# Attention and Mamba on one core: the result added up by DMA, the input normalised on ScalarE, weights folded once, 144 columns of a product on GpSimd

## The chip, the cores and the metric

The kernel runs on one core of a Trainium2 chip. A core has five engines, each with its own queue of instructions that it takes strictly in order: TensorE (PE in the profile; PEld is its loading of weights), VectorE (DVE), ScalarE (ACT), GpSimd (POOL) and SyncE (SP), which here only issues DMAs. The metric is the device time of one execution in microseconds (us). The kernel before took 8720.66 us, the median of three runs (8711.55 to 8721.42).

## The reference

The input x has 8 samples of 512 channels and 48 x 48 = 2304 positions, in float32. Two layers are added to it:

```
x = x + L0(gn(x))       # linear causal attention, 8 heads of 64 channels
x = x + L1(gn(x))       # four Mamba blocks over 4 groups of 128 channels
```

`gn` normalises groups of 16 channels by their mean and variance over all positions. L0 projects the normalised input to q, k and v and takes a running sum over the positions. L1 goes through the four channel groups one after the other; each gets the fused output of the one before added to its input:

```
x_i   = spx[i] + prev                       # 128 channels
xp, z = split(x_i @ Wi.T)                   # 256 channels each
xs    = silu(causal_conv4(xp))              # one filter of 4 taps per channel
delta, B, C = projections of xs             # 16 states
h_t   = exp(delta*A) * h_{t-1} + (delta*xs) * B_t     # the scan, per channel and state
y     = (sum_n h_t C_t + D*xs) * silu(z);  x_m = y @ Wo.T
fused = sigmoid(mean x_i) * x_i + sigmoid(mean max) * max(x_i, x_m)
prev  = fused                               # and the block's output
```

So the result for a channel group is x1 (the input plus attention) plus fused.

## The kernel before, in words

**Tiling.** The positions are cut into 6 chunks of LC = 384 columns. The attention of a sample is done in 4 passes of 128 output channels, 6 chunks each: 8 x 4 x 6 = 192 chunks (`chunk`). The Mamba part has 32 blocks (8 samples x 4 groups), each of 6 jobs (`Job`): 192 jobs. A job has 8 slots, and a slot treats 2 of the 16 states for 128 of the 256 channels (two groups of 64 channels, two states each, so that 128 partitions are full): 1536 slots.

**A slot.** The tile u holds 4 rows of 384 columns per partition. First u = B x (delta xs) is formed: DVE makes the first LC - TAIL = 256 columns (`product`, L867, from dxp, a copy in PSUM that ACT made at L840), POOL the last TAIL = 128 (`last_product`, L856). Then DVE scans the four rows (`scan`, L888), each with a decay that ACT has just computed into a PSUM bank (`decay`, L877). POOL multiplies all of u by C (`weigh`, L900), and PE sums the states into yp (`gather`, L916). The decays are made up to three ahead of the scans (`DEPTH`). POOL's part of the product is issued two slots ahead and DVE's one; u has five buffers.

**A job's preparation** (`prepare`): convolution (PE, L693) with the folded weights wk, SiLU on ACT, projections, delta by Softplus (ACT, L764). Delta is stored to DRAM (`spread`, L773), then multiplied in place by xs on POOL in two halves (L805), and stored again. From DRAM both are read back in the layout of the slots (dr, dxr), as are B and C (L797). The first half of L805 overwrites what the first store reads, so it waits for that DMA.

**Weights** (`weights`): before each of the 32 blocks the kernel loads the projection wi and the four taps, spread over the partitions, as wk, and POOL multiplies wk by wi for each tap (L539, 128 instructions), one every three half slots. ACT makes the table av (L536, L540).

**Passing on** (`pass_on`): when a block is done, chunk by chunk, fused is put together: ACT scales the stored maximum fu and the input xi (L654, L655), POOL adds them (L662) and adds fused to the next block's input (L667, or ACT at L665 where a new sample begins). Then POOL adds fused to x1, which was loaded as xo (L670), and the sum is stored to `out`. The last block of stream 1 has a path of its own on DVE (L630).

**Attention chunk.** In the first pass of a sample (o = 0) the chunk's input xn is loaded from x (`fetch`, issued when the chunk before starts), normalised on POOL in four instructions (L317), used by PE for the projections (L293), and stored for the three later passes, which load it normalised. The attention's output plus x (x1) is stored to a scratch tensor in DRAM.

**Order.** The schedule is written out by hand. Time is counted in half slots. Two streams of blocks (even and odd samples) take turns. At every half slot `beside` advances the side tasks that are due, each a generator whose `yield` says how many half slots later, or at which one, it goes on; `at(j)` means j half slots from the start of the chunk, and chunks start 16 half slots apart (11 in the ramp). `save` puts a store in a list, and `flush` issues it on SP at least two half slots later. The place of an instruction in its engine's queue is thus fixed when the program is built; when it runs depends on the waits of all that stands before it.

Of the kernel before, what the change touches and what calls it, by code (L numbers as in the profile page):

```python
# [9 lines left out]
F32 = mybir.dt.float32  # L10
BF16 = mybir.dt.bfloat16
AF = mybir.ActivationFunctionType
ALU = mybir.AluOpType
# [8 lines left out]
SLOTS = 8  # L22
TAIL = 128
BANKS = 6
# [26 lines left out]
def attention_then_mamba_kernel(  # L51
# [206 lines left out]
    def fetch(m):  # L258

        if m == len(parts):  # L260
            return
        b, o, c = parts[m]
        if (o, c) == (0, 0):
            xns[b] = dpool.tile([512, L], F32, tag="xn", name=f"xn_{b}", bufs=B)
            x1s[b] = dpool.tile([512, L], F32, tag="x1", name=f"x1_{b}", bufs=B)
        xn = apool.tile([P, 4, LC], F32, tag="xn", name=f"xn_{b}_{o}_{c}", bufs=2)
        src = (x[b] if o == 0 else xns[b]).rearrange("(t p) l -> p t l", p=P)
        nc.sync.dma_start(out=xn, in_=src[:, :, c * LC : (c + 1) * LC])
        fetched[m] = xn
# [3 lines left out]
    def chunk(m):  # L273
# [35 lines left out]
        if o == 0:  # L309
            yield at(-4), 0  # L310
            while b not in norms or m not in fetched:
                yield "1w", 0
            xn, norm = fetched.pop(m), norms[b]
            for ct in range(4):
                if ct:
                    yield at(ct - 4), 0
                nc.gpsimd.tensor_scalar(  # L317
                    xn[:, ct, :],
                    xn[:, ct, :],
                    norm[:, 0, ct : ct + 1],  # L320
                    norm[:, 1, ct : ct + 1],
                    ALU.mult,
                    ALU.add,
                )
            save(xns[b].rearrange("(t p) l -> p t l", p=P)[:, :, cols], xn)
# [165 lines left out]
        if c + 1 == NC:  # L491
# [4 lines left out]
            done[b, o] = norm  # L496

    class Stream:

# [10 lines left out]
        def weights(self):  # L510
# [6 lines left out]

            wk = wpool.tile([P, 4, 256], F32, tag=f"wk{z}", name=f"wk_{n}")
            nc.sync.dma_start(
                out=wk.rearrange("p k d -> p (k d)"), in_=wconv[s].to_broadcast([P, 1024])  # L520
            )
# [14 lines left out]
            nc.scalar.activation(av, av, AF.Exp)  # L536
            for k in range(4):
                yield "3", 0
                nc.gpsimd.tensor_tensor(wk[:, k, :], wk[:, k, :], wi[:, 0:256], ALU.mult)  # L539
            nc.scalar.mul(av, av, -1.0)  # L540
            self.scaled = True

        def move_on(self):

            if self.b is not None and self.s < 3:
                self.s += 1
                self.fresh = False
            else:
                self.b, self.s = self.samples.pop(0), 0
                self.fresh = True  # L550
            self.ready = 0
            self.block += 1
            self.n = f"{self.b}_{self.s}"
            self.state = small.tile(
                [P, 2, NS // 2, 2], F32, tag=f"state{self.z}", name=f"state_{self.n}", bufs=1
            )
            self.fsum = small.tile([P, NC], F32, tag=f"fsum{self.z}", name=f"fsum_{self.n}", bufs=1)
            self.fm = dpool.tile([P, L], F32, tag="fm", name=f"fm_{self.n}")
            self.w = self.coming

        def pass_on(self):
# [39 lines left out]
            def loads(c):  # L601
                fu = xb = xa = None
                cols = slice(c * LC, (c + 1) * LC)
# [3 lines left out]
                if old is not None:  # L607
                    fu = mpool.tile([P, LC], F32, tag="fu", name=f"fu_{old[2]}_{c}")
                    nc.sync.dma_start(out=fu, in_=old[3][:, cols])
                    xa = mpool.tile([P, LC], F32, tag="xo", name=f"xo_{old[2]}_{c}")  # L610
                    nc.sync.dma_start(out=xa, in_=x1s[old[0]][old[1] * P : (old[1] + 1) * P, cols])
                return fu, xb, xa

            if last and self.z:
# [19 lines left out]
                return  # L634
            now = loads(0)
            for c in range(NC):
# [12 lines left out]
                cols, icols = slice(c * LC, (c + 1) * LC), slice(3 + c * LC, 3 + (c + 1) * LC)  # L649
                fu, xb, xa = now  # L650
                if not last:
# [8 lines left out]
                if old is not None:  # L660
# [5 lines left out]
                    elif not last:  # L666
                        nc.gpsimd.tensor_tensor(xi[:, icols], xb, fu, ALU.add)  # L667
                    self.ready = c + 1
                    yield "1", 0
                    nc.gpsimd.tensor_tensor(xa, xa, fu, ALU.add)  # L670
                    save(out[old[0], old[1] * P : (old[1] + 1) * P, cols], xa)
                self.ready = c + 1

    class Job:
# [6 lines left out]
        def prepare(self):  # L681
# [120 lines left out]

            for h in range(2):
                yield "1", 0
                nc.gpsimd.tensor_tensor(delta[:, h, :], delta[:, h, :], xs[:, h, :], ALU.mult)  # L805
            yield "2", 0
            xsrc = spread("xscr")
# [227 lines left out]
    def begin(latest):  # L1035

        nonlocal begun, put
        while counted and begins[counted[0]] - 4 <= half_no[0]:
            tasks.append(Task(statistics(counted.pop(0))))
        while put < len(parts) and times[put] - 6 <= half_no[0]:  # L1040
            put += 1
            heads.append(Task(chunk(put - 1), before=heads[-1] if heads else None))
# [226 lines left out]
```

## Time and profile before

| | |
|---|---|
| median of three runs | 8720.66 us (8711.55 to 8721.42) |
| the profiled execution's own time | 8723.09 us |
| its span in the profile | 8721.0 us |
| mean granted TensorE clock | 0.964 |
| DMA | 1643 MB, 188 GB/s, SP's queue 69.1% of 16 engines |
| longest waits on SP's queue | 1187 us for L805, 832 us for L670 |
| POOL's waits at L805 | 235 us for the store of delta (80 times), 56 us booked on another DMA |

The span is the time from the first to the last instruction that the profile shows. A busy time is the time in which an engine had an instruction in work, and since PE pipelines its matmuls, its busy time is an upper bound. A line of a group says: line of the kernel, engine, operation, output and inputs with their shapes, count, busy time and mean duration of one in ns, and the idle time of the engine just before these instructions with what ended it. A line of the waits says who waited for whom, how long in total, how often, and the longest. A line of the stretches gives a window, its length, and the busy time of PE, PEld, DVE, ACT and POOL with the number of instructions, then the granted clock, the share of the DMA engines and GB/s.

### The profile page before, as it was taken

Reading aid. Unit: us, or ns where it says so; the run is one execution under the profiler, and the core shown is the slowest. Engines: PE = TensorE matmul, PEld = TensorE weight load, DVE = VectorE, ACT = ScalarE, POOL = GpSimd, SP = SyncE. Lnnn points to the kernel's source line nnn. Section 1 sums busy time; section 2 is a strip of 40 time slices with the busy share of each in tenths; the row PEclk is TensorE's granted clock in tenths of the full one; section 3 lists DMA queues with packets and bytes.
Section 4 is the critical chain, followed back from the end, with each engine's and each line's share of the span. In section 5 each row is a group of like instructions: output and inputs, shape, how many; then the busy total and the mean of one; then the engine's idle time right before and its main releaser. Section 6 shows DMA issues by size and latency. Waiting matters only on the chain. (4 is left out here: it accounts for less than half of the span.)

```text
span 8721.0 us, 124881 instructions
## 1 busy us (share of the span) xinstructions
PE 7774.7 (89%) x36482; PEld 3714.5 (43%) x36482; DVE 8072.2 (93%) x11078; ACT 6852.0 (79%) x14500; POOL 7834.3 (90%) x4343
## 2 busy tenths in 40 slices
PE   7899999988899999998889999999889999999965
PEld 4444444444444444444444444444444444444422
DVE  2899999999899999998899999999889999999998
ACT  2788888777788888877778888887777888888876
POOL 1789999999999999998998999998999889999998
PEclk9999999999999999999999999999999999999987
DMA  5667777776766777776676777776666667766665
GB/s 183 168 178 190 196 198 197 191 191 189 195 188 190 193 200 199 197 189 191 187 193 186 193 190 197 196 197 187 188 185 194 188 188 190 189 188 185 183 165 146
DMA packets 1002924, 1643.11 MB, mean 188 GB/s; under 512 B 138592, under 2 KB 797312, under 8 KB 1002240
## 3 DMA queue, kind: packets, MB, share of 16 engines
q1 hardware_dynamic: 1002240, 1635.13, 69.1%
q8 instruction: 290, 4.75, 0.2%
q14 instruction: 394, 3.23, 0.1%
HBM read 1309.06 MB, written 325.58 MB: 187 GB/s over the span
## 5 line engine op out<-in xcount | busy, mean ns | idle before, releaser
L888 DVE TENSOR_TENSOR_SCAN u<-bank,u 128x385 f32<-128x385 f32 (+1 forms) x6144 | 5455.4, 938 | 327.4 <-ACT bank L877 288.3
L900 POOL TENSOR_TENSOR u<-u,C 128x1536 f32<-128x1536 f32 x1536 | 4892.7, 3185 | 345.6 <-DVE u L888 186.9
L877 ACT ACTIVATE bank<-dr,av 128x385 f32<-128x385 f32 (+1 forms) x6144 | 3405.1, 578 | 671.0 <-DVE u L888 575.2
L916 PE MATMUL yp<-u,cst 128*64 128x384 f32 x12288 | 2417.7, 515 | 343.9 <-POOL u L900 259.6
L856 POOL TENSOR_TENSOR u<-B,dxr 128x512 f32<-128x512 f32 x1536 | 1969.9, 1283 | 17.5 <-DMA dxr<-xscr 15.4
L867 DVE TENSOR_TENSOR u<-B,dxp 128x1024 f32<-128x1024 f32 x1536 | 1835.0, 1195 | 9.7 <-ACT dxp L840 9.7
L293 PE MATMUL bank<-xn,wq_sb 128*128 128x384 f32 x4608 | 1725.8, 519 | 74.2 <-DVE u L888 33.0
L916 PEld LDWEIGHTS yp<-u,cst 128*64 128x64 f32 x12288 | 780.7, 139 | 1557.9 <-issue 871.9
L693 PE MATMUL bank<-xi,wk 128*128 128x384 f32 x3072 | 1110.7, 505 | 198.6 <-ACT kl L390 108.7
L293 PEld LDWEIGHTS bank<-xn,wq_sb 128*128 128x128 f32 x4608 | 867.4, 199 | 842.4 <-DVE u L888 140.0
L693 PEld LDWEIGHTS bank<-xi,wk 128*128 128x128 f32 x3072 | 558.8, 192 | 761.4 <-ACT kl L390 211.6
L805 POOL TENSOR_TENSOR delta<-delta,xs 128x384 f32<-128x384 f32 x384 | 385.7, 1005 | 361.8 <-DMA dscr<-delta 234.6
L305 ACT ACTIVATE ex<-bank,bqkv_sb 128x384 f32<-128x384 f32 x384 | 221.5, 577 | 505.3 <-PE bank L293 505.3
L877 ACT ACT_TABLE_LOAD x382 | 490.1, 1283 | 6.8
L845 ACT ACTIVATE yp<-xs,pv 128x384 f32<-128x384 f32 x384 | 223.6, 582 | 278.0 <-DVE yz L928 277.5
L934 PE MATMUL bank<-yz,wo 128*128 128x384 f32 x768 | 302.1, 510 | 24.4 <-DVE yz L928 17.3
L753 PE MATMUL bank<-dbc,wd 9*128 9x384 f32 x768 | 312.4, 527 | 3.7 <-ACT dbc L745 3.7
L704 PE MATMUL bank<-xi,wi 128*128 128x384 f32 x768 | 287.5, 495 | 9.7 <-ACT xs L729 9.7
L423 PE MATMUL bank<-cst,rdb 128*128 128x128 f32 x576 | 110.0, 304 | 200.9 <-DVE u L888 198.7
L740 PE MATMUL bank<-xs,wx 128*40 128x384 f32 x768 | 280.0, 487 | 2.7 <-ACT sm L457 2.7
L476 PE MATMUL bank<-sm,v 128*64 128x128 f32 x2304 | 257.1, 302 | 0.0
L729 ACT ACT_TABLE_LOAD x192 | 246.3, 1283 | 3.6 <-PE bank L693 0.2
(117 smaller groups left out, 7978.0 us busy)
## 6 DMA issues: line engine op xcount, KB each, us to landing
B<-scr SPq DMA_DIRECT2D x1536, 192.0 KB
C<-scr SPq DMA_DIRECT2D x1536, 192.0 KB
xn<-xn SPq DMA_DIRECT2D x192, 768.0 KB
dr<-dscr SPq DMA_DIRECT2D x768, 192.0 KB
dxr<-xscr SPq DMA_DIRECT2D x768, 192.0 KB
dscr<-delta SPq DMA_DIRECT2D x192, 384.0 KB
xscr<-delta SPq DMA_DIRECT2D x192, 384.0 KB
xn<-in_x SPq DMA_DIRECT2D x48, 768.0 KB
```

The costliest lines, as they stand in the source:

```text
L293: nc.tensor.matmul(ps, wq_sb[:, kt, j * 512 + o * P : j * 512 + (o + 1) * P], xn[:, kt, :], start=(kt == 0), stop=(kt == 3),)
L693: nc.tensor.matmul(xc, wk[:, k, h * P : (h + 1) * P], xi[:, c0 + k : c0 + k + LC], start=(k == 0), stop=(k == 3),)
L704: nc.tensor.matmul(zp, wi[:, 256 + h * P : 256 + (h + 1) * P], xi[:, c0 + 3 : c0 + 3 + LC], start=True, stop=True,)
L753: nc.tensor.matmul(vp, wd[32:41, h * P : (h + 1) * P], dbc[32:41, :], start=True, stop=True)
L805: nc.gpsimd.tensor_tensor(delta[:, h, :], delta[:, h, :], xs[:, h, :], ALU.mult)
L856: nc.gpsimd.tensor_tensor(u[:, :, :, 1 + LC - TAIL :], self.B[s % 4][:, :, cols].unsqueeze(2).to_broadcast(shape), self.dxr[s // 4][:, :, ...
L867: nc.vector.tensor_mul(u[:, :, :, 1 : 1 + LC - TAIL], self.B[s % 4][:, :, cols].unsqueeze(2).to_broadcast(shape), self.dxp.unsqueeze(1).to ...
L877: nc.scalar.activation(dA[:, cols], self.dr[h][:, g, cols], AF.Exp, scale=self.w[6][:, 2 * h + g, q + j : q + j + 1],)
L888: nc.vector.tensor_tensor_scan(u[:, j, g, cols], dA[:, cols], u[:, j, g, cols], 0.0, ALU.mult, ALU.add,)
L900: nc.gpsimd.tensor_tensor(u[:, :, :, 0:LC], u[:, :, :, 1:], self.C[s % 4].unsqueeze(2).to_broadcast([P, NG, 2, LC]), ALU.mult,)
L916: nc.tensor.matmul(self.yp[g * 64 : g * 64 + 64, 0:LC], pair_sum, u[:, j, g, 0:LC], start=False, stop=(s % 4 == 3 and j == NG - 1), skip_g ...
L934: nc.tensor.matmul(self.xm[:, 0:LC], self.w[2][:, h, :], self.yz[:, h, :], start=(h == 0), stop=(h == 1),)
```

## The change

Five things are done together.

1. TAIL is 144 instead of 128: POOL makes 144 columns of the product with B, DVE 240.
2. x1 is no longer kept in a scratch tensor but is stored in `out` itself. In `pass_on`, xo, its load, the addition L670 and its store are gone. Fused is written back over the stored maximum (fm), and after chunks 2 and 5 of a block one DMA, issued from POOL's queue, adds half of it (128 rows of 1152 columns) onto `out`. fm has 6 buffers instead of 4. The path of the last block stays.
3. The normalisation of xn is done by ACT (Identity with bias and scale) instead of POOL, at half slots -7, -7, -3 and -2 before the chunk instead of -4 to -1.
4. The folded weights of a group are stored in DRAM the first time, and later blocks load them instead of the taps; the four products are then left out.
5. Delta is multiplied by xs in one instruction instead of two; the steps after it keep their times.

```diff
-TAIL = 128
+TAIL = 144
...
-            x1s[b] = dpool.tile([512, L], F32, tag="x1", name=f"x1_{b}", bufs=B)
+            x1s[b] = out[b]
...
-            yield at(-4), 0
+            yield at(-7), 0
             while b not in norms or m not in fetched:
                 yield "1w", 0
             xn, norm = fetched.pop(m), norms[b]
-            for ct in range(4):
-                if ct:
-                    yield at(ct - 4), 0
-                nc.gpsimd.tensor_scalar(
+            for ct, when in enumerate((-7, -7, -3, -2)):
+                if when > -7:
+                    yield at(when), 0
+                nc.scalar.activation(
                     xn[:, ct, :],
                     xn[:, ct, :],
-                    norm[:, 0, ct : ct + 1],
-                    norm[:, 1, ct : ct + 1],
-                    ALU.mult,
-                    ALU.add,
+                    AF.Identity,
+                    bias=norm[:, 1, ct : ct + 1],
+                    scale=norm[:, 0, ct : ct + 1],
                 )
...
+            flat, known = wk.rearrange("p k d -> p (k d)"), s in folded
             nc.sync.dma_start(
-                out=wk.rearrange("p k d -> p (k d)"), in_=wconv[s].to_broadcast([P, 1024])
+                out=flat, in_=folded[s] if known else wconv[s].to_broadcast([P, 1024])
             )
...
-            for k in range(4):
+            if not known:
+                for k in range(4):
+                    yield "3", 0
+                    nc.gpsimd.tensor_tensor(wk[:, k, :], wk[:, k, :], wi[:, 0:256], ALU.mult)
+                folded[s] = dpool.tile([P, 1024], F32, tag="folded", name=f"folded_{s}")
+                save(folded[s], flat)
+            else:
                 yield "3", 0
-                nc.gpsimd.tensor_tensor(wk[:, k, :], wk[:, k, :], wi[:, 0:256], ALU.mult)
...
-            self.fm = dpool.tile([P, L], F32, tag="fm", name=f"fm_{self.n}")
+            self.fm = dpool.tile([P, L], F32, tag="fm", name=f"fm_{self.n}", bufs=6)
...
-                    xa = mpool.tile([P, LC], F32, tag="xo", name=f"xo_{old[2]}_{c}")
-                    nc.sync.dma_start(out=xa, in_=x1s[old[0]][old[1] * P : (old[1] + 1) * P, cols])
...
-                    self.ready = c + 1
-                    yield "1", 0
-                    nc.gpsimd.tensor_tensor(xa, xa, fu, ALU.add)
-                    save(out[old[0], old[1] * P : (old[1] + 1) * P, cols], xa)
+                    save(old[3][:, cols], fu)
                 self.ready = c + 1
+                if old is not None and c % half == half - 1:
+                    yield "6", 0
+                    rows, cols = slice(old[1] * P, (old[1] + 1) * P), slice((c + 1 - half) * LC, (c + 1) * LC)
+                    nc.gpsimd.dma_start(
+                        out=out[old[0], rows, cols], in_=old[3][:, cols], accum_op=ALU.add
+                    )
...
-            for h in range(2):
-                yield "1", 0
-                nc.gpsimd.tensor_tensor(delta[:, h, :], delta[:, h, :], xs[:, h, :], ALU.mult)
-            yield "2", 0
+            yield "1", 0
+            nc.gpsimd.tensor_tensor(delta, delta, xs, ALU.mult)
+            yield "3", 0
...
-        while put < len(parts) and times[put] - 6 <= half_no[0]:
+        while put < len(parts) and times[put] - 9 <= half_no[0]:
```

More of the change, by code (lines that the diff above doesn't have):

```diff
@@ L496, in chunk @@
             done[b, o] = norm
+    folded = {}
     class Stream:
@@ L601, in loads @@
             def loads(c):
-                fu = xb = xa = None
+                fu = xb = None
                 cols = slice(c * LC, (c + 1) * LC)
@@ L609, in loads @@
                     nc.sync.dma_start(out=fu, in_=old[3][:, cols])
-                    xa = mpool.tile([P, LC], F32, tag="xo", name=f"xo_{old[2]}_{c}")
-                    nc.sync.dma_start(out=xa, in_=x1s[old[0]][old[1] * P : (old[1] + 1) * P, cols])
-                return fu, xb, xa
+                return fu, xb
             if last and self.z:
@@ L634, in pass_on @@
                 return
-            now = loads(0)
+            now, half = loads(0), NC // 2
             for c in range(NC):
@@ L649, in pass_on @@
                 cols, icols = slice(c * LC, (c + 1) * LC), slice(3 + c * LC, 3 + (c + 1) * LC)
-                fu, xb, xa = now
+                fu, xb = now
                 if not last:
```

## The prediction

> **What bounds the kernel now.** I read the busy times by stretch first, then who waits for whom, then the groups of instructions by line, then one stall in order of time. The page's first part gives the totals:
>
> ```profile
> PE 7774.7 (89%) x36482; PEld 3714.5 (43%) x36482; DVE 8072.2 (93%) x11078; ACT 6852.0 (79%) x14500; POOL 7834.3 (90%) x4343
> ```
>
> Two engines are nearly full, and a mean over the span doesn't say which one sets the pace. So I cut the span at the changes of the busy digits. Two of the stretches, all engines first (PE, PEld, DVE, ACT, POOL), and then the weighing product L900 alone, whose count is the number of slots:
>
> ```profile
> 1852.00:2400.00 548.00, 477.92 (x2231) 223.87 (x2226) 494.07 (x681) 421.42 (x895) 505.96 (x304) 0.96 0.71 192
> 2400.00:4032.00 1632.00, 1488.71 (x7132) 716.93 (x7131) 1570.23 (x2160) 1336.66 (x2824) 1510.40 (x819) 0.99 0.72 193
> ...
> 1852.00:2400.00 548.00, 301.47 (x95) 0.96 0.71 192
> 2400.00:4032.00 1632.00, 953.22 (x300) 0.99 0.72 193
> ```
>
> There are two kinds of stage. Three stretches (1852 to 2400, 4032 to 4577, 6120 to 6665 us: 1638 us, 283 slots) hold 138 of the 192 input normalisations L317 (93.2 us); I call them normalising. Four others (from 436 to 8208 us: 6134 us, 1125 slots) I call plain; ramp and end hold the rest. A slot takes 5.45 us in the plain stages and 5.79 us in the normalising ones, 0.34 us more. DVE's work is the same in both (5.22 and 5.20 us a slot), POOL's is 5.02 and 5.32. The normalisation alone is 93.2/283 = 0.33 us of POOL a slot. So the plain stages run on DVE, 95.8% busy, and the normalising ones on POOL. POOL's own waits there make that firm:
>
> ```profile
> POOL delta L805 <- DMA xr<-in_x: 21.9, 9, 6.5
> POOL delta L805 <- DMA dscr<-delta: 13.2, 2, 6.9
> ```
>
> These are from the first normalising stretch: 35 us in which POOL, whose queue is in order, stands at L805 until the stored delta has been read out. With 506 us busy, POOL is occupied for 541 of 548 us. How such a wait gets to the scans is seen in order of time (start, length, instruction, idle before and its releaser):
>
> ```profile
> 6187.11 1.00 POOL L805 TENSOR_TENSOR delta<-delta,xs 128x384 f32<-128x384 f32 x1 [6.31 <-DMA xr<-in_x]
> 6191.29 2.53 PE L916 MATMUL yp<-u,cst 128*64 128x384 f32 x8 [3.80 <-POOL u L900]
> 6202.89 5.49 PE L693 MATMUL bank<-xi,wk 128*128 128x384 f32 x8 [3.48 <-POOL xi L667]
> 6208.96 0.48 ACT L390 COPY kl<-bank 128x384 f32<-128x384 f32 x1 [5.31 <-PE bank L386]
> 6210.34 0.96 DVE L888 TENSOR_TENSOR_SCAN u<-bank,u 128x385 f32<-128x385 f32 x1 [4.47 <-ACT bank L877]
> ```
>
> POOL is late, PE's queue stands behind POOL, ACT's behind PE, and DVE waits for a decay. So most of what the next line books on ACT begins elsewhere:
>
> ```profile
> DVE u L888 <- ACT bank L877: 288.3, 213, 4.5
> ```
>
> **The change part by part.** The rows for the prices:
>
> ```profile
> L900 POOL TENSOR_TENSOR u<-u,C 128x1536 f32<-128x1536 f32 x1536 | 4892.7, 3185 | 345.6 <-DVE u L888 186.9 <-issue 39.9 <-DMA B<-scr 31.6
> L856 POOL TENSOR_TENSOR u<-B,dxr 128x512 f32<-128x512 f32 x1536 | 1969.9, 1283 | 17.5 <-DMA dxr<-xscr 15.4 <-DMA B<-scr 2.1
> L867 DVE TENSOR_TENSOR u<-B,dxp 128x1024 f32<-128x1024 f32 x1536 | 1835.0, 1195 | 9.7 <-ACT dxp L840 9.7
> L670 POOL TENSOR_TENSOR xo<-xo,fu 128x384 f32<-128x384 f32 x186 | 187.8, 1010 | 0.0
> L317 POOL TENSOR_SCALAR xn<-xn,norm_a 128x384 f32<-128x384 f32 x192 | 128.5, 673 | 84.3 <-DMA xn<-in_x 62.8 <-DMA x<-xr 11.9 <-PE bank L293 9.3
> L659 ACT ACTIVATE xb<-xb,norm_m 128x384 f32<-128x384 f32 x144 | 100.3, 697 | 0.0
> L539 POOL TENSOR_TENSOR wk<-wk,wi 128x256 f32<-128x256 f32 x128 | 94.8, 743 | 6.9 <-DMA wk<-in_wconv 3.7 <-DMA av<-in_alog 3.1
> ```
>
> *TAIL 144.* DVE's product loses 64 of 1024 elements. Between L928 (384 elements, 550 ns) and L867 an element costs 1.01 ns: 64.5 ns a slot, 99 us over 1536 slots. POOL's part gains 64. Between L856 and L900 an element costs 1.86 ns, between L805 (384 elements, 1005 ns) and L856 2.17: 119 to 139 ns, I take 125, 192 us. L840 copies 32 columns less of each of 384 tiles; by L390 (384, 477 ns) and L840 (512, 582 ns) that is 26 ns, 10 us of ACT. The Trainium skill, GPSIMD Engine Reference, section 4.1, speaks against this step: elementwise work with two inputs belongs on VectorE, being about twice as slow on GpSimd. The rows say the same (125 against 64.5 ns): taken alone, the sum is +192 us on POOL for -99 us on DVE, a loss wherever POOL is the bound.
>
> *Result by DMA.* The 186 additions L670 go (188 us of POOL), with 186 loads of xo. The 186 stores of xo become stores of fu. 62 accumulating DMAs (31 blocks, two halves) are added on POOL's queue. The trace has no DMA issued from POOL. From below, a store issued by SP takes 0.34 us (out<-xo); from above, POOL's longest instruction takes 3.19. I take 1.0, the addition that it replaces: 62 us (21 to 198). A page has a price: DMA: Bandwidth & Descriptors, section SWDGE vs HWDGE vs iDMA, says that an accumulating DMA must be issued from GpSimd, where software writes its descriptors, and its first table gives about 1 us to the first byte; by an estimate from that page the sum would be 62 us too; no run here shows it. What it waits for are three fu stores. They are flushed two halves after the last addition, and the DMA comes six halves after it: four halves, 11 us, for a store, against at most 7.5 us that POOL waited for a DMA outside the ramp. I put the wait at nothing; behind it stand the next weighing product and, through PE and ACT, the scans. SP loses its waits for xo (832 us, 185 times), mostly to the next wait in its queue; I count nothing. The bytes grow by 2 to 4% (fu written, x1 read and written in DRAM). Bursts of 590 KB take 3.1 us at the mean 188 GB/s and can lengthen the delta waits: from 0 to 62 x 3.1 us if each met one; a wait fills about 6.5 of a job's 44 us, so 28 us, and 12 us as my value, since not each delays all.
>
> *Weights folded once.* 20 of 128 products L539 stay (stream 1 begins before stream 0 has stored): 108 x 743 ns = 80 us of POOL. The load of wk keeps its 512 KB; five stores of that size are new. The table is complete nine halves sooner, and nothing in the plain stages waits for it: nothing.
>
> *One product for delta.* 192 of 768 elements (1283 + 256 x 1.86 = 1758 ns) for 384 of 1005: 48 us of POOL. The first half waits where it waited before; the wait at L805 stays.
>
> *Normalisation on ACT.* POOL loses 128 us. ACT gains 192 instructions; L659 has the same operands and takes 697 ns: 134 us. No table load stands at the lines of Identity (L364, L659), so none is added. They are issued three halves earlier, two of four together. The load has been issued nine halves before (25 us) in the normalising stages, where none was waited for. In the ramp it is four halves, and all 62.8 us of waiting for xn lie there; but the loads of 112.7 and 127.7 us landed at 119.1 and 134.4, and ACT gets to that place at 122 and 137, so I count nothing. What is queued behind the new instructions is the next decay, with three decays (2.6 us of scans) as cover.
>
> **The sum.** POOL: -188 -128 -80 -48 +192 = -252 us busy, and 62 us of issuing. DVE: -99. ACT: +124.
> Normalising stages: they return to the plain pace, 0.34 x 283 = -95 us, if ACT takes its 138 x 0.70 = 96 us for nothing. ACT's work there rises from 4.43 to 4.77 us in a slot of 5.45, 87%, above any stage in this trace (82%). Its price on the scans lies between 0 (ACT sat idle for 384 us there) and 96; the rows point both ways, so I take half, 48: net -47.
> Plain stages: DVE gains 0.065 a slot. POOL gains 0.12 (xo), 0.055 (wk), 0.03 (delta) and pays 0.125 and 0.04 (45 DMAs): 0.04. So 0.04 to 0.065 x 1125 = 48 to 73 us; I take 60. At the same rate the normalising stages give 14 and the end 5. Bursts: +12. Ramp: 0 (its pace, 15 us a chunk between 115 and 160 us, is PE's).
> -47 -60 -14 -5 +12 = -114 us, from the profiled execution's own 8723.1 us (span 8721.0): **8609 us**. The median of the runs shown, 8720.7, is 2.4 us from it, which is left out.
>
> **Rivals.**
> (a) ACT becomes the bound of the normalising stages: all 96 us fall on the scans, the plain stages gain 48. -95 + 96 - 48 + 12 = -35: 8688. For it: 288 us of DVE waits are booked on ACT, in 18 waits of 1.6 us and more in each normalising stretch. Against: ACT itself waited there for PE and POOL (in the last one 37 us at L305, 16 at L665), and that shrinks.
> (b) POOL's relief goes further: ACT's price is 0, the plain stages gain 73, and some of the 288 us goes with the late POOL: -95 -73 -14 -5 = -187: 8536.
> (c) Slower: the accumulating DMA blocks POOL's queue until the store has landed. POOL's relief of 252 us over 62 DMAs is 4.1 us each; from there on POOL has more to do than before. At 7.5 us of wait and 1.0 of issue it is 62 x 8.5 - 252 = +275 us on POOL, half of it taken up by POOL's other idle time: 8723 + 137 = 8860. For it: L805 shows that POOL stands still so. Against: the 11 us above.
> (d) The edits take effect but cancel, within 17 us: 8720.
>
> **How the numbers follow.** Forecast 0.52, (b) 0.16, (a) 0.14, (d) 0.06, (c) 0.12. The range reaches over (b) and (a) and takes in part of the unknown DMA price: 8525 to 8705. A measurement of this kernel tells 0.2% (17 us) from no change. Faster by more: the forecast, (a) and (b), 0.82; within: 0.06; slower: 0.12.
>
> **What would show it.** L867's successor near 1130 ns, L856's near 1408, normalisations on ACT near 700, delta's product near 1760. POOL busy near 7580, DVE 7973, ACT 6976. The normalising stretches at about 5.5 to 5.6 us a slot, the plain ones near 5.40, with DVE over POOL in both. (a) shows as DVE waits at L888 for L877 well over 33 us in a normalising stretch; (c) as POOL's idle before its DMA line. I am wrong if the normalising stages keep 5.8 us a slot, or if POOL's issue takes more than 4 us.

## The result and the profile after

The changed kernel took 8829.0 us, the median of four runs (8816.6 to 8862.9), beside 8721.0 us before: a ratio of 1.013, 95% interval 1.0097 to 1.0163. It is 108 us slower where 114 us less was forecast. The busy times came out nearly as worked out. The first part of the page of the kernel after (its profiled execution: 8816.6 us, span 8814.9):

```profile
PE 7783.5 (88%) x36482; PEld 3728.8 (42%) x36482; DVE 7983.5 (91%) x11078; ACT 6950.4 (79%) x14692; POOL 7679.1 (87%) x3727
```

DVE was to have 7973 us and has 7984; ACT 6976, and 6950; POOL 7580 and some issuing, and 7679, of which the DMAs take 50. So what failed is not the work but the waiting: DVE's idle time rose from 649 to 831 us.

The first normalising stage and the plain one behind it, at their new places, all engines first, then the weighing product alone (its line is now L907), whose count is the slots:

```profile
1862.00:2405.00 543.00, 476.45 (x2274) 228.04 (x2275) 498.25 (x693) 454.40 (x957) 480.65 (x233) 0.98 0.72 195
2405.00:4011.00 1606.00, 1453.33 (x6862) 699.64 (x6864) 1495.96 (x2076) 1282.09 (x2723) 1437.71 (x694) 0.97 0.71 189
...
1862.00:2405.00 543.00, 305.18 (x96) 0.98 0.72 195
2405.00:4011.00 1606.00, 918.92 (x289) 0.97 0.71 189
```

543/96 = 5.66 us a slot in the normalising stage: better than before, but not the plain pace. 1606/289 = 5.56 in the plain one: worse than before, with less work on DVE and on POOL. Measured from scan to scan over all stages (288 normalising and 1056 plain slots), the kernel after takes 1646 and 5877 us for them, the kernel before 1666 and 5775. The plain stages lose 102 us, the ramp 16 (first scan at 246.1 instead of 229.9 us).

The groups that changed, of the kernel after:

```profile
L863 POOL TENSOR_TENSOR u<-B,dxr 128x576 f32<-128x576 f32 x1536 | 2190.8, 1426 | 27.0 <-DMA dxr<-xscr 23.2 <-DMA ksum<-before 1.3 <-DMA out<-xr 1.0
L874 DVE TENSOR_TENSOR u<-B,dxp 128x960 f32<-128x960 f32 x1536 | 1743.9, 1135 | 116.4 <-ACT dxp L847 108.9 <-DMA B<-scr 3.5 <-DMA out<-xr 3.0
L812 POOL TENSOR_TENSOR delta<-delta,xs 128x768 f32<-128x768 f32 x192 | 349.3, 1819 | 393.4 <-DMA dscr<-delta 243.2 <-ACT bank L884 36.9 <-DMA xr<-in_x 32.6
L317 ACT ACTIVATE xn<-xn,norm_a 128x384 f32<-128x384 f32 x192 | 129.5, 700 | 6.3 <-DVE norm_a L202 2.7 <-DMA xn<-in_x 2.4
L678 POOL DMA_DIRECT2D out<-fm x62 | 49.6, 799 | 0.0
```

Every mean duration is near the forecast's (1408, 1130, 1760, 700 ns, 1 us); POOL doesn't wait at its DMA line (idle 0.0); and one line has an idle time that it did not have: DVE's product L874 waits 109 us for dxp, before 10. The waits of the kernel after, DVE, ACT and SP, say why:

```profile
DVE u L895 <- ACT bank L884: 366.2, 205, 5.0
DVE u L874 <- ACT dxp L847: 108.9, 67, 5.9
...
ACT dxp L847 <- DMA dxr<-xscr: 145.4, 84, 4.4
...
SPq L167 <- POOL fu L667: 1163.5, 184, 10.2
SPq L167 <- ACT dbc L753: 955.0, 192, 8.7
```

ACT's copy dxp waits for the load of dxr, 84 times. In the kernel before it was 4 times:

```profile
ACT dxp L840 <- DMA dxr<-xscr: 6.1, 4, 5.3
```

That load is in SP's queue, and SP now waits 1164 us for POOL's addition fu, at L167, the line that issues stored results. A long wait there is no loss by itself, since SP waited 832 us for xo and 1187 us for L805 before; what counts is which loads stand behind it. One such place in order of time, SP's queue, then POOL, ACT and DVE:

```profile
3483.66 0.38 SPq L781 DMA_DIRECT2D xscr<-delta  x1
3492.27 0.32 SPq L167 DMA_DIRECT2D fm<-fu  x1
3492.69 1.26 SPq L792 DMA_DIRECT2D dr<-dscr  x2
3494.05 1.19 SPq L805 DMA_DIRECT2D B<-scr  x2
3495.29 0.58 SPq L253 DMA_DIRECT2D xs<-in_x  x1
3495.97 1.25 SPq L792 DMA_DIRECT2D dxr<-xscr  x2
...
3488.10 3.18 POOL L907 TENSOR_TENSOR u<-u,C 128x1536 f32<-128x1536 f32 x1
3491.24 1.00 POOL L667 TENSOR_TENSOR fu<-fu,xi 128x384 f32<-128x384 f32 x1
...
3500.95 0.56 ACT L847 COPY dxp<-dxr 128x480 f32<-128x480 f32 x1 [3.00 <-DMA dxr<-xscr]
...
3501.54 1.15 DVE L874 TENSOR_TENSOR u<-B,dxp 128x960 f32<-128x960 f32 x1 [2.74 <-ACT dxp L847]
```

The product with delta is stored at 3483.66, and the loads of dr and dxr are to follow. But a store of fu stands between, and POOL finishes fu at 3492.24 only; for 8.2 us SP, in order, issues nothing. In the kernel after a store fm<-fu stands at just this place in 121 of 192 jobs, and SP stands before it for 1008 us in all. In the kernel before nothing stood there in 188 of 192. The cause is in `prepare`: ahead of the loads of dr there is a `flush()` (L810 before, L817 after) that issues every store that is pending, however young (the rule of two half slots, as the section on the kernel before has it, holds only for the flush of `beside`). Before, the addition of xo and its store came one half slot later, behind that point; now the store of fu is handed over ahead of it.

### The profile page after: what moved, and what is told of

The parts are those of the page before. It is cut to its first block, busy times and chain, and to the rows that moved or that the text cites. A ratio compares the mean times of both kernels' runs of the same rounds, so it can differ in the third digit from the quotient of the medians.

```text
span 8814.9 us, 124537 instructions
## 1 busy us (share of the span) xinstructions
PE 7783.5 (88%) x36482; PEld 3728.8 (42%) x36482; DVE 7983.5 (91%) x11078; ACT 6950.4 (79%) x14692; POOL 7679.1 (87%) x3727
## 5 line engine op out<-in xcount | busy, mean ns | idle before, releaser
L907 POOL TENSOR_TENSOR u<-u,C 128x1536 f32<-128x1536 f32 x1536 | 4901.5, 3191 | 531.4 <-DVE u L895 302.2
L863 POOL TENSOR_TENSOR u<-B,dxr 128x576 f32<-128x576 f32 x1536 | 2190.8, 1426 | 27.0 <-DMA dxr<-xscr 23.2
L874 DVE TENSOR_TENSOR u<-B,dxp 128x960 f32<-128x960 f32 x1536 | 1743.9, 1135 | 116.4 <-ACT dxp L847 108.9
L701 PE MATMUL bank<-xi,wk 128*128 128x384 f32 x3072 | 1159.4, 523 | 270.6 <-ACT kl L389 198.3
L701 PEld LDWEIGHTS bank<-xi,wk 128*128 128x128 f32 x3072 | 579.2, 198 | 852.7 <-ACT kl L389 309.3
L812 POOL TENSOR_TENSOR delta<-delta,xs 128x768 f32<-128x768 f32 x192 | 349.3, 1819 | 393.4 <-DMA dscr<-delta 243.2
L884 ACT ACT_TABLE_LOAD x382 | 490.1, 1283 | 6.7
L847 ACT COPY dxp<-dxr 128x480 f32<-128x480 f32 x384 | 213.9, 557 | 145.4 <-DMA dxr<-xscr 145.4
L712 PE MATMUL bank<-xi,wi 128*128 128x384 f32 x768 | 289.6, 497 | 17.2 <-ACT xs L737 17.2
L935 DVE TENSOR_TENSOR yz<-yp,sz 128x384 f32<-128x384 f32 x384 | 213.9, 557 | 75.9 <-PE yp L923 75.9
```

Source lines behind the costliest of these rows:

```text
L701: nc.tensor.matmul(xc, wk[:, k, h * P : (h + 1) * P], xi[:, c0 + k : c0 + k + LC], start=(k == 0), stop=(k == 3),)
L712: nc.tensor.matmul(zp, wi[:, 256 + h * P : 256 + (h + 1) * P], xi[:, c0 + 3 : c0 + 3 + LC], start=True, stop=True,)
L812: nc.gpsimd.tensor_tensor(delta, delta, xs, ALU.mult)
L863: nc.gpsimd.tensor_tensor(u[:, :, :, 1 + LC - TAIL :], self.B[s % 4][:, :, cols].unsqueeze(2).to_broadcast(shape), self.dxr[s // 4][:, :, ...
L874: nc.vector.tensor_mul(u[:, :, :, 1 : 1 + LC - TAIL], self.B[s % 4][:, :, cols].unsqueeze(2).to_broadcast(shape), self.dxp.unsqueeze(1).to ...
L884: nc.scalar.activation(dA[:, cols], self.dr[h][:, g, cols], AF.Exp, scale=self.w[6][:, 2 * h + g, q + j : q + j + 1],)
```

## The experiments

Three theories were on the table first. Q: the store of fu, pushed out by the flush, holds up SP's loads of delta's products. D: the 62 accumulating DMAs cost the time, by their traffic or on POOL's queue. A: the normalisations cost it on ACT. Each ratio below is to the kernel before as it ran beside that experiment; it took 8718 to 8731 us there, so a difference between two experiments is good to some 10 us.

**1. The store handed over one half slot later**, where the store of xo had been (e1_store_later):

```diff
                         nc.gpsimd.tensor_tensor(xi[:, icols], xb, fu, ALU.add)
+                    self.ready = c + 1
+                    yield "1", 0
                     save(old[3][:, cols], fu)
```

> The changed kernel, with the store of fu saved one half slot later, as the store of xo was; nothing else moves. Theory Q (the fu store stands in SP's queue in front of the dr, B and dxr loads in 121 of 192 jobs, and SP waits there for POOL's addition): the store goes behind the loads in all but two jobs, DVE's waits for dxp fall from 109 us to under 20, SP's wait for the fu addition from 1164 to under 700, and the time falls to 8610 to 8680 us. Theory D (the accumulating DMA is what costs) and theory A (ACT's normalisations are what costs): 8800 us or more, waits for dxp as in the changed kernel.

8765.3 us (ratio to before 1.0046, 1.003 to 1.0063). DVE's waits for dxp are gone but for one of 6 us and SP's for fu fell to 207 us, as Q has it; but only 64 us came back, and the time lies in neither theory's range. Something else is lost here (run 16).

**2. The counter-test in the kernel before:** the addition of xo and its store one half slot earlier (e2_before_store_earlier).

```diff
                     self.ready = c + 1
-                    yield "1", 0
                     nc.gpsimd.tensor_tensor(xa, xa, fu, ALU.add)
```

> The kernel before, with the addition L670 and the store of xo one half slot earlier; none of the change's five parts is in it. Theory Q: the xo store now stands in front of the loads in 121 jobs, waits for dxp appear (80 us or more, from 10), and the kernel is slower by 80 to 200 us: 8800 to 8920 us. Theories D and A: nothing in it costs anything, 8700 to 8740 us.

9424.0 us (1.0799, 1.0783 to 1.0815): one line, and 700 us. The direction is Q's, the size far beyond what was expected. The waits of DVE, ACT and SP in that kernel:

```profile
DVE u L866 <- ACT dxp L839: 475.1, 116, 8.2
...
ACT dxp L839 <- DMA dxr<-xscr: 543.3, 121, 8.4
...
SPq L167 <- POOL xo L669: 1313.9, 185, 9.0
```

It is the same chain as in the kernel after, with 3.7 times the wait at dxp (543 against 145 us). The order of time says why, SP's queue first and then POOL:

```profile
3106.96 0.38 SPq L772 DMA_DIRECT2D xscr<-delta  x1
3115.44 0.34 SPq L167 DMA_DIRECT2D out<-xo  x1
...
3111.26 1.00 POOL L662 TENSOR_TENSOR fu<-fu,xi 128x384 f32<-128x384 f32 x1
3112.22 1.28 POOL L855 TENSOR_TENSOR u<-B,dxr 128x512 f32<-128x512 f32 x1
3113.45 0.99 POOL L667 TENSOR_TENSOR xi<-xb,fu 128x384 f32<-128x384 f32 x1
3114.41 1.00 POOL L669 TENSOR_TENSOR xo<-xo,fu 128x384 f32<-128x384 f32 x1
```

The store waits for the addition of xo, which POOL finishes 3.2 us after that of fu; in the kernel after it waits for fu alone. SP's stop is as long in both (8.1 and 8.4 us in the mean), but it ends later: 2.8 us after the start of slot 5 of the job before, as against 0.1 (medians over jobs 12 to 179; slots are counted from 0). The load of dxr is issued at 6.4 as against 3.5 us, and at -1.7 in the kernel before.

**3. The kernel after without the flush** (e3_no_flush):

```diff
             yield first - 7, 0
-            flush()
             steps(0)
```

> The changed kernel without the forced flush of all stores ahead of the dr loads; each store then goes out two half slots after it was saved. The fu store is saved where the changed kernel saves it. Theory Q: no job but one has a store in front of its loads, so the time is as in e1, 8610 to 8680 us. Theories D and A: 8800 us or more.

8668.5 us (0.9937, 0.992 to 0.9953), 54 us faster than the kernel before: Q is confirmed, and so is its size, 160 us. D and A wanted 8800 us or more. The traces show the loss at its place. From the start of slot 5 of the job before to a job's first scan, the 121 jobs with the store in front take 18.8 us in the kernel after and 17.3 in this run (+182 us over all 121), 23.5 in run 2 and 17.2 in the kernel before (+754); the other 70 jobs take 17.5 to 17.6 in all four. SP still waits 559 us for fu here, but never directly ahead of the loads of dr.

**4. The kernel after without the 62 DMAs** (e4_no_accumulation):

> The changed kernel without its 62 accumulating DMAs; fused is not added to the output, so this part of the result is left out. Theory Q: the fu store is still in front of the loads, so at most the 50 us of POOL and the transfers go: 8760 to 8830 us. Theory D: 8700 us or less. Theory A: 8800 us.

8799.6 us (1.0089, 1.0074 to 1.0105), 29 us less than with them, and the two intervals overlap. D falls as the main cause.

**5. The control: the kernel before without the flush** (e5_before_no_flush):

> The kernel before, without the flush ahead of the loads of dr. It is the control for the kernel after without that flush (8668 us). Theory Q (the flush hurts only where a store of fu or xo is pending at that point, and in the kernel before two of 192 jobs have one): 8700 to 8735 us, no change. Rival R (holding back pending stores pays in any case, and the rest of the change gives nothing): 8650 to 8690 us, and as fast as the kernel after without the flush.

8719.5 us (1.0, 0.9991 to 1.0009). The flush is harmless as long as nothing is pending; the loss comes from both together.

The next question was what each part of the change is worth once the flush is out of the way. **6. TAIL back at 128** (e6_no_flush_tail_128):

> The kernel after without the flush (8668 us), and with TAIL back at 128 columns. DVE's product gets 64 elements a slot back (+99 us busy on DVE), POOL's loses them (-192 us). Theory T (the plain stages gained nothing because a slot there now needs POOL's time, waits and the 62 issues included, as much as DVE's): 8580 to 8650 us. Rival U (DVE still sets the pace of the plain stages, and 144 columns earn their 0.065 us a slot): 8720 to 8770 us. If neither engine alone decides (both wait in turn on decays and on PE): within 20 us of 8668.

8653.5 us (0.9932, 0.9915 to 0.9948): neither theory T's number nor U's, but the third case of the expectation, within 20 us of run 3. The interval overlaps that of run 3, so the 15 us aren't settled; the 99 us that DVE gets back and the 192 that POOL loses about cancel.

**7. The normalisation on POOL again**, at the old places (e7_no_flush_norm_on_pool):

> The kernel after without the flush (8668 us), with the input normalised on POOL again, at the old places and with the old lead of the loads. Theory N (ACT's normalisation brings the gain of the three normalising stages, about 73 us, and costs the 16 us of the ramp): 8668 + 73 - 16 = 8725 us, between 8700 and 8745, with the first scan back at 230 us. Rival M (those stages gained from POOL's other reliefs, the additions of xo and the folded weights): 8640 to 8665 us, the ramp's 16 us gained and nothing lost.

8718.8 us (0.9999, 0.9989 to 1.001), as theory N has it: all the other parts together bring nothing. The first scan came at 236.1, not 230 us.

**8. Only the first sample on POOL** (e8_no_flush_ramp_on_pool):

> The kernel after without the flush (8668 us), with the 48 normalisations of the first sample on POOL again at their old places, the other 144 on ACT. Theory N (the ramp is 16 us longer since ACT's normalisations stand in its queue waiting for their loads and for exp(av)): first scan near 230 us, 8652 us. Rival: the ramp's loss is of PE's pace or of the later first store, and the first scan stays at 246 us: 8668 us.

8654.1 us (0.9926, 0.9911 to 0.994), within the interval of run 3, and the first scan at 242.5, not 230: N's account of the ramp explains 4 of 16 us.

**13. The normalisation alone, in the kernel before** (e13_norm_on_act_alone), with the same lines of the diff for L317 and the loads:

> The kernel before with one part of the change, the input normalised on ACT at the new places. Theory N (that part is the whole net gain; all others together cancel once the flush is out of the way, since the kernel after without the flush and with the normalisation on POOL gave 8719 us, as before): 8670 us, between 8655 and 8690, with the three normalising stages near 5.55 us a slot and the ramp 10 to 16 us longer. Rival (it needs POOL's other reliefs to pay): 8695 to 8720.

8651.6 us (0.9912, 0.9897 to 0.9926), 79 us faster than before on that chip. It is the whole gain of the change, and more. This edit moves the normalisations to ACT and also three half slots earlier, with their loads; which of the two brings the gain wasn't tested apart. Its normalising stages take 5.55 us a slot (before 5.79), its plain ones 5.46, its first scan comes at 241.6. So 12 of the 16 us of the ramp come with it, though run 8 gave only 4 back; what the others are stays open.

**9 to 11: what is a microsecond worth?** Three kernels each take some work from one engine and leave that part of the result out. For PE `range(3)` in place of `range(4)` in the projections, for DVE `1 + LC - 16` as the end of the scan, for POOL `LC - 20` columns in `weigh`.

> The kernel after without the flush (8668 us), leaving out the last of the four matmuls of each attention projection (L293), so a quarter of those sums is missing. PE loses about 1170 matmuls of 0.38 us: 445 us busy, 0.28 us a slot. Theory P (PE, 5.02 of 5.47 us a slot busy, sets the pace of the plain stages, so neither DVE's nor POOL's relief could show): the plain stages fall by at least half of that, to 5.33 us a slot or less, and the time to 8440 us or less. Theory V (DVE sets it, as the prediction said): plain stages within 0.05 of 5.47, the time above 8590 us but for the ramp, which is PE's (up to -30 us).

> The kernel after without the flush (8668 us), leaving the last 16 of 384 columns of every scan undone, so that the result is not the reference's there. At 2.3 ns a column DVE loses 4 x 37 ns a slot, 226 us busy. Theory V (DVE sets the pace of the plain stages): at least 0.11 us a slot less there, 8500 us or less. Theory P (PE) or O (POOL): less than 0.05 us a slot, above 8590 us. If all three share the pace (each waits for the next in turn): near 0.07, 8560 us.

> The kernel after without the flush (8668 us), leaving the last 20 of 384 columns unweighed (no product with C there), so that the result is not the reference's. At 1.86 ns an element POOL loses 80 x 1.86 = 149 ns a slot, 229 us busy. Theory O (POOL with its waits sets the pace): at least 0.11 us a slot less, 8500 us or less. Theory V or P: less than 0.05, above 8590 us. Sharing: near 8560 us.

The first parts of the three pages, and of run 3's, which is the last line:

```profile
PE 7467.9 (87%) x35330; PEld 3498.3 (41%) x35330; DVE 7980.6 (93%) x11078; ACT 6958.4 (81%) x14692; POOL 7677.6 (89%) x3727
```
```profile
PE 7677.1 (90%) x36482; PEld 3694.2 (43%) x36482; DVE 7790.7 (91%) x11078; ACT 6930.3 (81%) x14692; POOL 7676.6 (90%) x3727
```
```profile
PE 7708.2 (90%) x36482; PEld 3700.4 (43%) x36482; DVE 7970.6 (93%) x11078; ACT 6939.8 (81%) x14692; POOL 7451.2 (87%) x3727
```
```profile
PE 7760.3 (90%) x36482; PEld 3718.9 (43%) x36482; DVE 7987.1 (92%) x11078; ACT 6945.8 (80%) x14692; POOL 7679.1 (89%) x3727
```

| taken away | us of work | time | gain | a us is worth |
|---|---|---|---|---|
| PE | 292 | 8620.6 (0.9884, 0.9869 to 0.9898) | 48 (8 of it in the ramp) | 0.16 |
| DVE | 196 | 8557.9 (0.9817, 0.9798 to 0.9836) | 111 | 0.56 |
| POOL | 228 | 8585.5 (0.9845, 0.983 to 0.9859) | 83 | 0.36 |

No engine sets the pace alone; the gain is shared, DVE having the largest share. That is the third case of the expectations of runs 10 and 11, at 8558 and 8585 us for 8560; run 9 rules out PE, for which 8440 us or less were expected. The four times of run 10 lie in two pairs, near 8543 and 8572 us, so DVE's price is 0.49 to 0.64. ACT's price wasn't tested. The plain stages take 5.38 us a slot with less DVE work, 5.42 with less on POOL, 5.45 with less on PE, 5.47 in run 3.

**12. TAIL 128 and the first sample on POOL together** (e12_tail_128_and_ramp):

> The kernel after without the flush (8668 us), with TAIL back at 128 columns (alone: 8653.5) and the first sample normalised on POOL (alone: 8654.1). If the two gains are of different stretches (the ramp, and the stages after it), they add: 8640 us, between 8630 and 8648. If both come from POOL's queue in the same place: 8653 us.

8650.6 us (0.9924, 0.9909 to 0.9939): the two small gains don't add up.

By these prices the work taken off DVE (85 us by the two pages) and off POOL (155) should bring the kernel of run 3 some 100 us, and the ramp takes 16 back; 54 came. ACT's 94 us more have no price in this sum. **14 to 16** look for the rest: the product for delta in two halves again, no accumulating DMAs, and the store of fu later.

```diff
-            yield "1", 0
-            nc.gpsimd.tensor_tensor(delta, delta, xs, ALU.mult)
-            yield "3", 0
+            for h in range(2):
+                yield "1", 0
+                nc.gpsimd.tensor_tensor(delta[:, h, :], delta[:, h, :], xs[:, h, :], ALU.mult)
+            yield "2", 0
```

> The kernel after without the flush (8668 us), with the product for delta in two instructions of 1.0 us at two places again instead of one of 1.82 us. POOL's busy time rises by 36 us; by what an us of POOL was worth in the last runs (83 us for 228) that alone is +13. Theory L (the single long instruction holds up POOL's queue, and scans behind it, more than it saves): 8625 to 8655. Rival (only the busy time counts): 8675 to 8690.

8638.1 us (0.9894, 0.988 to 0.9909): 30 us less than run 3 (37 by the ratios), with 24 us more work on POOL. This is the fastest complete kernel of the study.

> The kernel after without the flush (8668 us), leaving out the 62 accumulating DMAs, so fused is not added to the output. Theory D2 (their issuing and traffic use up the part of the gain that POOL's reliefs should bring, some 45 us): 8615 to 8635. Rival (as with the flush, about 30 us, or less, the issuing alone: 50 us of POOL at 0.36): 8638 to 8655.

8615.0 us (0.9869, 0.985 to 0.9888): the DMAs cost 53 us.

> The kernel after without the flush (8668 us), with the store of fu handed over one half slot later, where the store of xo was. Theory S (SP's 559 us of waiting for fu, in 185 places, still delay loads): 8625 to 8655. Rival (once the store doesn't stand ahead of the loads of dr, its place doesn't matter): 8660 to 8676.

8772.1 us (1.0051, 1.0036 to 1.0066), nearly as in run 1: with the later store the flush makes no difference, and beside run 3 the later store costs 104 us. Both theories were wrong here. The trace shows where: slots 3 to 5 of every sixth job. These are the jobs in whose slot 1 SP issues the loads of the next block's weights.

| slots 3 to 5, us | every sixth job (28) | the other jobs (140) |
|---|---|---|
| before | 17.43 | 15.58 |
| after | 18.89 | 15.27 |
| 3, no flush | 18.69 | 15.40 |
| 14, delta in halves | 17.26 | 15.26 |
| 15, no accumulation | 17.27 | 15.26 |
| 16, store later | 21.15 | 15.69 |

POOL's queue in one of these jobs of run 16, in order of time:

```profile
2917.09 1.67 POOL L864 TENSOR_TENSOR u<-B,dxr 128x576 f32<-128x576 f32 x1
2925.67 1.80 POOL L814 TENSOR_TENSOR delta<-delta,xs 128x768 f32<-128x768 f32 x1 [6.91 <-ACT bank L885]
2927.43 3.17 POOL L908 TENSOR_TENSOR u<-u,C 128x1536 f32<-128x1536 f32 x1
```

and SP's queue there with its wait, the accumulating DMA as POOL issues it, and its size and time to landing:

```profile
2912.93 0.44 SPq L525 DMA_DIRECT2D wo<-in_wout  x1
2918.75 0.33 SPq L527 DMA_DIRECT2D wx<-in_wxp  x1
...
2922.75 0.38 SPq L783 DMA_DIRECT2D dscr<-delta  x1
...
SPq L527 <- DMA xn<-xn: 5.3, 1, 5.3
...
2908.81 0.90 POOL L680 DMA_DIRECT2D out<-fm  x1
...
out<-fm POOLq DMA_DIRECT2D x1, 576.0 KB, 9.2
```

POOL stands 6.9 us at delta's product. The wait is booked on an ACT instruction that had long been done, so the DMA that reads delta out is the likelier releaser. That DMA isn't slower here: in the 28 jobs the product starts 3.0 us after SP issues the store of delta in the mean, in runs 3, 15 and 16 alike. But the store is issued later, 18.9 us after the job's first scan in run 16, 17.3 in run 3 and 16.5 in run 15. Ahead of it in SP's queue stand the weights' loads, and one of them, L527, waits for the load of xn: 5.3 us here, 2.3 in the same job of run 15. The accumulating DMA is under way then and has landed, at 2918.0, before delta is stored. That it slows the load of xn is likely and not shown by itself.

Its place matters, as the traces show. In run 3 it is issued in slot 0 of 12 of the 28 jobs and in the slot before in 15. Beside run 15, which has none, slots 3 to 5 take 2.7 us more in the 12 (20.68 as against 17.96) and 0.3 more in the 15 (17.00 and 16.74). In run 16 it is issued in slot 0 in 27, and both groups take 3.9 us more than in run 15. The store moved too in run 16, so the two aren't separated.

**17 and 18** were to move the accumulating DMAs 12 half slots later, away from there (`yield "18"` for `yield "6"`), alone and with the other cures.

> The kernel after without the flush (8668 us), with each accumulating DMA issued 12 half slots later. Theory K (in every sixth job one of them, 576 KB, falls in the same two slots as the loads of the next block's weights and the store of delta, so delta's product stands 7 us at the head of POOL's queue; slots 3 to 5 of those 28 jobs take 18.69 us against 15.40 in the others): 8615 to 8640 us, nearly as without the DMAs (8615), and those slots near 17.3 us. Rival (its bytes or its issue cost wherever it stands): within 12 us of 8668.

> The kernel after without the flush (8668 us), with the accumulating DMAs 12 half slots later, the product for delta in two halves again (alone -30), TAIL at 128 columns (alone -15) and the first sample normalised on POOL (alone -14). If the four are independent: 8668 - 40 - 30 - 15 - 14 = 8570 us. If the later DMAs and the halves of delta cure the same wait (every sixth job's slots 3 to 5 came to 17.27 us without the DMAs and to 17.26 with the halves), and the ramp's gain is lost again as it was with TAIL at 128: 8600 to 8625 us. At 8640 or more, the wait isn't what they share.

8881.1 us (1.0188, 1.0174 to 1.0202) and 8865.9 (1.0165, 1.0152 to 1.0179). They did not do what their expectations say: the planner reads only the first digit of a wait, so that "18" meant one half slot and the DMAs came five half slots earlier. There the last of their three stores isn't issued yet (in chunks 2 and 5 the stored maximum is added in place of fused), and that store, which overwrites what the DMA reads, waits for it at the head of SP's queue. SP's waits of run 17:

```profile
SPq L167 <- DMA out<-fm: 873.8, 62, 15.7
```

That is 14.1 us for each DMA. Rival (c) had feared such a wait for POOL; here it is SP's. The theory they were made for stays untested.

## Why the prediction was wrong, point by point

- **What bounds the kernel.** The normalising stages were read rightly: run 13 takes 0.23 of the 0.34 us a slot that the prediction put down to the normalisation. "The plain stages run on DVE" was half right: DVE's price is the highest (0.56), not 1, and POOL's is not 0 but 0.36. In the plain stages alone the profiled execution of run 10 (8543 us) gains 99 us of 135 us of work, 0.73, an estimate that spreads the 196 us evenly over the slots; run 11 gives 0.37 there.
- **The step that failed: the result by DMA.** "They are flushed two halves after the last addition" and "SP loses its waits for xo (832 us, 185 times), mostly to the next wait in its queue; I count nothing". In `prepare` a flush issues pending stores at once, and the place that the store of fu got in SP's queue is ahead of dr and dxr. Cost: 160 us (run 3 against the kernel after) of the 220 us between forecast (8609) and result (8829). The prediction named the queue and did not write down what stands behind each store in it.
- **Its other terms.** Issuing: 0.80 us each (1.0 taken). Waiting of the DMA on POOL: none, as said. Bursts: 12 us were taken of a range up to 190; without the DMAs 29 us less with the flush, and 53 without it, issuing included. The way was another one: in one job of six the store of delta is issued later, and its reading out doesn't take longer.
- **One product for delta.** "48 us of POOL": 36 were saved, and the single instruction of 1.82 us costs 30 us in the end (run 14). They come back in slots 3 to 5 of every sixth job (18.69 to 17.26 us, 40 us over the 28). Busy time was counted, and not how long POOL's queue is shut in one piece; that this length is the reason is likely, not shown.
- **Folding and TAIL.** The folding moved its work as worked out (20 products of 0.73 us left). For TAIL the sum of -99 on DVE and +192 on POOL can be priced now: -55 + 69 = +14; run 6 says 15 (4 by the ratios), which isn't clear of its uncertainty. The Trainium skill, GPSIMD Engine Reference, section 4.1, prefers VectorE for a two-input product, as about twice as slow on GpSimd; here the 64 elements cost POOL 143 ns a slot (1426 less 1283) and saved DVE 60 (1195 less 1135), 2.4 times, so the rows agree in the direction and go somewhat further. The prediction took 125 and 64.5; in run 15, without the DMAs, POOL's figure is 134 (1417 ns).
- **Normalisation on ACT.** -47 and a share of -14 were forecast for the normalising stages; run 13 gives -66 there, run 3 -72. One table load was added after all (1.3 us, behind 23 us of waiting for the first xn). ACT's price was put at 48 us; the 0.10 us a slot that run 13 still lies above its plain pace are 28. The ramp was put at 0 and cost 16, of which 12 come with the normalisation (run 13).
- **The sum.** Without the flush the change brings -54 instead of -114: normalising stages -72 (-61 forecast), plain stages +7 (-60), ramp +17 (0), the first 12 jobs +2, end -9 (-5); the forecast's +12 of bursts belongs to no stage. The plain stages' +7 hold most of the 53 us of the DMAs and of the 30 of delta's product. The two may overlap, since each cure alone brings the slots of the table to 17.3 us; no run has both.
- **The rivals.** (a)'s sign stayed away: DVE's waits for a decay in the first normalising stretch fell from 29.3 to 26.0 us. (Its "18 waits of 1.6 us and more" are a mean; single ones there last 0.2 to 3.9 us.) (b) had ACT's work for nothing, and 28 us of its 96 remain. (c), the one on the slower side, named a wait behind the accumulating DMA on POOL. The slower side came true by another queue and another instruction, a plain store, so its 0.12 was no foresight of this.

What stays open: which part of run 16's 104 us is the place of the store and which that of the DMAs, which moved with it; the ramp's 16 us; and whether DMAs placed away from the loads of xn and the weights would recover the 53 us, as the 15 jobs of run 3 suggest.

## What to carry to other kernels

Where a store moves, write down the queue that issues it, entry by entry: what its wait is, and which loads stand behind it; an in-order queue turns one store that comes a half slot too early into lost time for an engine that has nothing to do with it. Work that is taken from an engine is worth the share that an elasticity test gives it (here 0.16, 0.36 and 0.56 us per us), not 0 or 1, and one long instruction in place of two can cost more than the busy time that it saves (30 us here). Try the parts of a bundled change alone: here one of five carried the whole gain.

## What the runs showed of the hardware

- One addition and its store, one half slot earlier in the queues of POOL and SP, cost the kernel before 700 us of 8720 (run 2).
- An accumulating DMA of 128 rows of 4.6 KB, from DRAM to DRAM, takes POOL 0.80 us to issue and lands after a median of 7.7 us (6.3 in run 3). The Trainium skill, DMA: Bandwidth & Descriptors, section SWDGE vs HWDGE vs iDMA, has such a DMA's descriptors written by software on GpSimd; the 0.80 us on POOL, as against 0.3 to 0.6 for SP's issues, agree with that.
- The granted TensorE clock was lower where more was waited: 0.965 in run 3, 0.948 in run 17, 0.934 in run 2, where PE was busy for 8007 us with the same 36482 matmuls that take 7760 in run 3. How the clock is granted, and what this costs, isn't shown.
